# Gate matmuls of two batches as seven block products, and one phase of pairs at the end

## The chip, the core and the metric

The kernel runs on one core of a Trainium2 chip. TensorE (PE; its weight loads are PEld) multiplies into eight PSUM banks; VectorE (DVE), ScalarE (ACT) and GpSimd (POOL) work on SBUF, the first two on PSUM as well; SyncE (SP) issues most transfers. Each engine takes its instructions in the order of its own queue, and a transfer that has to wait holds up those behind it on the queue that issues it. The metric is the time of one execution on the device in microseconds.

## What is computed

The layer works on 32 batches of 512 nodes with 256 channels. With h = relu(layernorm(x)) of one batch:

```python
hc = relu(bn1(conv1(h)))                  # 1x1 convolution over the channels
x_conv = relu(bn2(conv2(hc)) + h)         # 17 taps along the nodes
s = h @ w_se.T + b_se                     # 3 features
A = exp(-dist(s)) * adj
x_nmp = A @ relu(h @ w_msg.T + b_msg)
gi = concat(x_conv, x_nmp) @ w_ih.T + b_ih
gh = h @ w_hh.T + b_hh
r = sigmoid(gi_r + gh_r); z = sigmoid(gi_z + gh_z)
n = tanh(gi_n + r * gh_n)
out = x + (1 - z) * n + z * h
```

The gates are three outputs of 256 channels (r, z, n) from three inputs of 256 channels (h, x_nmp, x_conv). In blocks of 128 channels that is 6 output blocks times 6 input blocks for every batch. Everything is float32.

## The kernel before

The 32 batches are two groups of 16. Conv2 goes through a Fourier transform: each batch is cut into 8 windows, the windows of a group's 16 batches fill 128 rows, and there are 40 `product` units per group that multiply spectra with the transformed taps. The stages, in program order:

- `first_part(0)`: statistics, normalisation, transposition of x to h (`hT`, stored as HD), conv1, forward transform into `xf`; beside it the taps are transformed and stored (WD). The weights of the gates, `wih` and `whh`, are loaded here in six transfers, one per batch.
- nodes of group 0: `message` (`pm`), `features`, `factors` (`psl`, `psr`), `affinity` (`pd`, the exponential, the transposed adjacency `at`, and their product `A`), `aggregate` (`pn`), `save_nmp` (ND). The 40 products of the group (`py`) lie between these steps, two or three per batch.
- `first_part(1)`, the same without the taps. Its order on each engine is the written one. Per batch it takes `rstd` by a power on GpSimd (L237), and it loads x on GpSimd's queue.
- rest of group 0, with the products of group 1 between: per batch the inverse transform (`freq_to_windows`, `pc` at L426), `gates_rz` and `gate_n` (`pg`, `pgh`, `pgi` at L436), `finish` (`po`, the output).
- last phase: for each batch of group 1 the nodes of the next batch and the gates of this one, between each other.

Where the order isn't fixed by hand, a scheduler at build time orders instructions by the program's order and by the buffers that are free. A gate block is one chain of matmuls into a fresh bank: for r and z six of them (two for each of hT, nmp and xconv), for n two and four in two banks. ScalarE takes the sigmoid out of the bank; VectorE and ScalarE make n and the blend. All gate weights stay in SBUF from the first stage on.

In the nodes phases the pool that holds the adjacency and `A` has one buffer of each.

## Time and profile before

| | |
|---|---|
| time, median of 3 runs | 2080.53 us (2076.18 to 2081.81) |
| profiled execution | 2081.35 us, span 2079.6 us |
| granted TensorE clock, mean | 0.988 |
| busy: PE, DVE, ACT, POOL | 2032.1, 909.1, 550.2, 285.9 us |
| stages, roughly from the chain in order of time | first 0 to 184; nodes and products 184 to 505; first 505 to 620; rest and products 620 to 1262; nodes and rest 1262 to 2080 |

A row of instructions gives line, engine, operation, output<-inputs, shapes, count; then busy time and the mean of one in ns, and the idle time of the engine ahead of them with what ended it. A matmul in float32 leaves two rows, so counts of TensorE are twice the number of matmuls. In the timeline a row starts with its start and length in us; in brackets stands the idle time ahead of it and who ended it. Rows of stretches give the busy time and count for PE, PEld, DVE, ACT and POOL, then the granted clock, the share of the DMA engines and GB/s.

### The profile page before, as it was taken

To read this page: it belongs to the slowest core of one execution; us is meant where nothing else is said; L and a number is where in the kernel's file an instruction comes from. 1 tells how busy PE (TensorE), PEld (TensorE's weight loads), DVE (VectorE), ACT (ScalarE), POOL (GpSimd) and SP (SyncE) were. 2 spreads that over 40 slices of the span, in tenths; PEclk is the share of its full clock that TensorE was granted. 3 is DMA by queue.
4 is the path that set the end of the run, shared out by engine and by line. 5 is a ranking of instruction groups with operands and counts; after the bars stand their busy time and mean duration, and the time that the engine had idled before them with its cause. 6 is when DMAs were issued, how large, how long until landed. Compare 5 with 4: busy or idle time off the path is not lost.

```text
span 2079.6 us, 20881 instructions
## 1 busy us (share of the span) xinstructions
PE 2032.1 (98%) x7616; PEld 1231.3 (59%) x7616; DVE 909.1 (44%) x1877; ACT 550.2 (26%) x898; POOL 285.9 (14%) x331
## 2 busy tenths in 40 slices
PE   7989999998999999999999999999999999999998
PEld 5666677675985555655556555555555555555554
DVE  7874666666962222321232223344444333333443
ACT  2544333332342111111111111222223222222231
POOL 2321333333211121221212100000000000000000
PEclk9997999999999999999999999999999999999999
DMA  8997887886554334453435451223333322222200
GB/s 214 320 267 197 231 217 229 237 219 209 170 171 129 123 120 128 144 171 95 131 124 155 144 134 51 50 74 76 84 79 89 86 70 70 70 70 70 70 30 20
DMA packets 222581, 277.47 MB, mean 133 GB/s; under 512 B 12959, under 2 KB 187871, under 8 KB 222479
## 3 DMA queue, kind: packets, MB, share of 16 engines
q1 hardware_dynamic: 205071, 227.30, 39.7%
q10 hardware_dynamic: 12224, 31.86, 4.0%
q0 software_dynamic: 5184, 16.98, 3.1%
q8 instruction: 61, 1.00, 0.2%
q14 instruction: 41, 0.34, 0.1%
HBM read 181.71 MB, written 94.37 MB: 133 GB/s over the span
## 4 chain that ended last, share of the span: by engine, by line
PE 90%; DVE 4%; DMA 2%; issue 1%; ACT 1%; POOL 0%; SPq 0%; DVEq 0%; POOLq 0%; ACTq 0%
PE pg L436 32%; PE pgi L436 11%; PE pn L396 10%; PE py L314 9%; PE pm L348 6%; PE pc L426 5%; PE pgh L436 5%; PE pc L267 3%; PE px L281 2%; PE pd L382 2%; PE po L479 1%; PE pw L212 1%; DVE stats L232 1%; PE phT L254 1%; DMA x<-in_x_dram 1%
## 5 line engine op out<-in xcount | busy, mean ns | idle before, releaser
L436 PE MATMUL pg<-nmp,wih 128*128 128x512 f32 x512 | 240.8, 592 | 0.0
L436 PE MATMUL pg<-hT,whh 128*128 128x512 f32 x512 | 240.6, 592 | 0.0
L436 PE MATMUL pg<-xconv,wih 128*128 128x512 f32 x512 | 240.6, 592 | 0.0
L462 DVE SCALAR_TENSOR_TENSOR n<-pgh,vec,rz 128x512 f32<-128x512 f32 x64 | 47.8, 747 | 428.3 <-PE pgh L436 428.3
L451 ACT ACTIVATE rz<-pg,brz 128x512 f32<-128x512 f32 x128 | 87.9, 687 | 541.3 <-PE pg L436 536.1
L396 PE MATMUL pn<-A,msg 128*128 128x512 f32 x512 | 227.7, 598 | 2.7 <-DVE A L388 2.7
L436 PEld LDWEIGHTS pg<-xconv,wih 128*128 128x128 f32 x512 | 97.3, 190 | 122.5 <-issue 122.5
L436 PEld LDWEIGHTS pg<-nmp,wih 128*128 128x128 f32 x512 | 97.2, 190 | 122.0 <-issue 121.5
L319 DVE COPY y<-py 128x256 f32<-128x256 f32 x78 | 31.5, 418 | 314.6 <-PE py L314 314.4
L396 PEld LDWEIGHTS pn<-A,msg 128*128 128x128 f32 x512 | 96.9, 192 | 120.4 <-issue 113.2
L436 PEld LDWEIGHTS pg<-hT,whh 128*128 128x128 f32 x512 | 97.2, 191 | 108.2 <-issue 104.3
L314 PE MATMUL py<-wt,both 128*128 128x256 f32 x624 | 148.1, 380 | 0.0
L306 POOL TENSOR_TENSOR both<-xf 128x256 f32<-128x256 f32 x78 | 60.6, 776 | 618.7 <-PE py L314 573.4
L387 DVE STREAM_TRANSPOSE at<-adj 128x512 f32<-128x512 f32 x128 | 134.3, 1083 | 10.8 <-DMA adj<-in_adj_dram 10.4
L348 PE MATMUL pm<-wmsg,hT 128*128 128x259 f32 x512 | 132.4, 413 | 0.0
L314 PEld LDWEIGHTS py<-wt,both 128*128 128x128 f32 x624 | 116.8, 190 | 24.6 <-issue 11.3
L348 PEld LDWEIGHTS pm<-wmsg,hT 128*128 128x128 f32 x512 | 123.5, 327 | 13.2 <-issue 11.4
L464 ACT ACTIVATE n<-n,vec 128x512 f32<-128x512 f32 x64 | 46.2, 722 | 318.2 <-DVE n L463 318.2
L426 PEld LDWEIGHTS pc<-back,yt 120*128 120x128 f32 x1024 | 119.5, 192 | 17.7 <-issue 17.7
L436 PE MATMUL pgh<-hT,whh 128*128 128x512 f32 x256 | 121.9, 598 | 0.0
L426 PE MATMUL pc<-back,yt 120*128 120x80 f32 (+1 forms) x1024 | 118.3, 273 | 2.6 <-DMA yt<-yd 2.6
L267 PE MATMUL pc<-w,hT 128*128 128x256 f32 x512 | 119.7, 388 | 0.6 <-DVE hT L255 0.6
(89 smaller groups left out, 2529.4 us busy)
## 6 DMA issues: line engine op xcount, KB each, us to landing
wt<-wd SPq DMA_DIRECT2D x160, 256.0 KB, 5.5
adj<-in_adj_dram SPq DMA_DIRECT2D x128, 256.0 KB, 5.1
yd<-y ACTq DMA_DIRECT2D x80, 384.0 KB, 5.8
yt<-yd SPq DMA_DIRECT2D x64, 480.0 KB, 6.6
hT<-hd SPq DMA_DIRECT2D x48, 512.0 KB, 3.8
wd<-wst SPq DMA_DIRECT2D x64, 320.0 KB, 5.5
x<-in_x_dram SPq DMA_DIRECT2D x38, 512.0 KB, 4.4
hd<-hT SPq DMA_DIRECT2D x32, 512.0 KB, 4.7
```

The source lines that it names most:

```text
L267: nc.tensor.matmul(p[:, j, :], HT[b][:, ic, c * P : (c + 1) * P], w1[:, ic, :], start=(ic == 0), stop=(ic == DC - 1))
L281: nc.tensor.matmul(p[:, j * 2 * L : (j + 1) * 2 * L], H1[b][:, c0 + j, ic * P : (ic + 1) * P], fwd, start=True, stop=True)
L306: nc.gpsimd.tensor_tensor(both[:, 0], re, im, op=ALU.add)
L314: nc.tensor.matmul(dst, v[:, ic, :], w[:, ic, :], start=(ic == 0), stop=(ic == DC - 1))
L348: nc.tensor.matmul(p[:, : D + NS], chunk(HT[b][:, ic, :], c), wmsg[:, ic, :], start=(ic == 0), stop=(ic == DC - 1))
L387: nc.vector.transpose(at.rearrange("p (j k) -> p j k", k=32), ADJ[b].rearrange("p j (q c) -> p c j q", c=NC)[:, mc])
L396: nc.tensor.matmul(p, MSG[b][:, mc, dc * P : (dc + 1) * P], A[b][:, mc, :], start=(mc == 0), stop=(mc == NC - 1))
L426: nc.tensor.matmul(p[:, t0:t1], YT[b][w][:, oc * P : (oc + 1) * P], back[:, u0 : u0 + t1 - t0], start=(w == 0), stop=(w == W - 1), skip_gr ...
L436: nc.tensor.matmul(p, w, v, start=(i == 0), stop=(i == len(terms) - 1))
L451: nc.scalar.activation(RZ[b][:, g, :], p, AF.Sigmoid, bias=brz[:, g : g + 1], scale=1.0)
L462: nc.vector.scalar_tensor_tensor(n, ph, b_hn[:, i : i + 1], RZ[b][:, i, :], op0=ALU.add, op1=ALU.mult)
L464: nc.scalar.activation(n, n, AF.Tanh, bias=b_in[:, i : i + 1], scale=1.0)
```

## The change

Two things change together.

**Gates of a pair.** Two batches are taken together. For one gate (256 output channels) and one source (256 input channels) the weights are 2 x 2 blocks a11, a12, a21, a22, and the operand is 2 x 2 blocks as well: input half by batch, each 128 x 512. Instead of 8 block products the kernel makes the seven of Strassen's method in Winograd's form: four sums of weight blocks (S1 to S4) and four differences of operand blocks take the place of single blocks in them. The products of the three sources h, nmp and xconv go into the same bank one after the other, since their sums are combined in the same way. The combination of the seven is partly done by accumulation: a bank that holds Q1 is copied out (`p1`) and goes on to Q1 + Q2; a bank with Q6 is read (`u2` = Q1 + Q6), goes on to Q6 + Q7, is read again (`u3`), and goes on to Q6 + Q7 + Q4. For n, the part of h and the part of the other two sources stay apart, in two banks each.

The differences of operands are made by GpSimd (`sums`, 4 for each source and pair). The weight sums are made once by GpSimd (`combine_weights`), stored to DRAM (WS), and loaded when the pairs begin.

**Order of the phases.** The nodes of group 1 follow `first_part(1)`, with the 40 products of group 1 spread over its first 13 batches; `save_nmp` stores all 32 batches. After that the early pools are closed, and one phase in written order runs the 16 pairs: load, inverse transform, gates, blend, output. A pair's output lies inside the next pair's `gates_rz`.

```diff
-    load_weights = [partial(nc.sync.dma_start, wih[:, i], w_ihT[i * P : (i + 1) * P]) for i in range(2 * DC)]
-    load_weights += [partial(nc.sync.dma_start, whh[:, i], w_hhT[i * P : (i + 1) * P]) for i in range(DC)]
-    load_weights += [
+    load_weights = [
...
+    def combine_weights():
+        sources = [w_hhT, w_ihT[D:], w_ihT[:D]]
+        for k, src in enumerate(sources):
+            w = pools["sums"].tile([P, DC, G], FP, tag="wraw", name=f"wraw_{k}")
+            nc.sync.dma_start(w, src.rearrange("(c p) o -> p c o", p=P))
+            w = w.rearrange("p c (g i o) -> p c g i o", i=2, o=P)
+            a11, a21, a12, a22 = w[:, 0, :, 0], w[:, 0, :, 1], w[:, 1, :, 0], w[:, 1, :, 1]
+            t = pools["sums"].tile([P, 7, 3, P], FP, tag="wsum7", name=f"wsum7_{k}")
+            for dst, a in ((A11, a11), (A12, a12), (A22, a22)):
+                nc.gpsimd.tensor_copy(t[:, dst], a)
+            nc.gpsimd.tensor_tensor(t[:, S1], a21, a22, op=ALU.add)
+            nc.gpsimd.tensor_tensor(t[:, S2], t[:, S1], a11, op=ALU.subtract)
+            nc.gpsimd.tensor_tensor(t[:, S3], a11, a21, op=ALU.subtract)
+            nc.gpsimd.tensor_tensor(t[:, S4], a12, t[:, S2], op=ALU.subtract)
+            nc.sync.dma_start(WS[k], t)
...
+    def load_pair(p):
+        HP[p] = pools["ops"].tile([P, 8, N], FP, tag="hp", name=f"hp_{p}")
+        NP[p] = pools["ops"].tile([P, 7, N], FP, tag="np", name=f"np_{p}")
...
+            nc.sync.dma_start(HP[p][:, j:4:2], HD[b])
+            nc.sync.dma_start(NP[p][:, j:4:2], ND[b])
...
+                nc.sync.dma_start(t, YD[g][w : w + W // 2].rearrange("w r d -> r w d"))
...
+    def sums(t, keep):
+        t3 = 7 if keep else B12
+        sub = ALU.subtract
+        for dst, a, b in ((4, B12, B11), (5, B22, 4), (6, B21, 5), (t3, B22, B12)):
+            nc.gpsimd.tensor_tensor(t[:, dst, :], t[:, a, :], t[:, b, :], op=sub)
...
+    def into(bk, q, o, ks, terms, first):
+        for i, k in enumerate(ks):
+            nc.tensor.matmul(bk, sw[:, k, q, o, :], terms[k][q], start=(first and i == 0), stop=(i == len(ks) - 1),
+                             skip_group_check=True)
...
+        for o in range(2):
+            b1[o] = bank(f"pg1_{p}_{o}")
+            into(b1[o], Q1, o, ks, terms, True)
+            p1[o] = temp("p1", f"{p}_{o}")
+            nc.scalar.copy(p1[o], b1[o])
+        for o in range(2):
+            b2[o] = bank(f"pg2_{p}_{o}")
+            into(b2[o], Q6, o, ks, terms, True)
+            u2[o] = temp("u2", f"{p}_{o}")
+            nc.vector.tensor_add(u2[o], p1[o], b2[o])
+        for o in range(2):
+            into(b1[o], Q2, o, ks, terms, False)
+            sigmoid(b1[o], o, 0, 0)
+        between(0)
+        for o in range(2):
+            into(b2[o], Q7, o, ks, terms, False)
+            u3[o] = temp("u3", f"{p}_{o}")
+            nc.vector.tensor_add(u3[o], p1[o], b2[o])
+        between(1)
...
+        pair(Q5, x3, True)
+        scaled(x3[0], u3[0], u3[1], 1, 1)
+        closing(x3[1], 1, 1)
+        pair(Q4, x2, False)
+        scaled(x2[0], p1[0], p1[1], 1, 0)
+        closing(x2[1], 1, 0)
+        pair(Q3, x3, False)
+        scaled(x3[0], u2[0], u2[1], 0, 1)
+        closing(x3[1], 0, 1)
+        for i, j in ((0, 0), (1, 1), (1, 0), (0, 1)):
+            blend(i, j)
...
+            with phase("nodes"):
+                nodes(0, xf, GB)
+            with phase("first", "sums"):
+                combine_weights()
                 xf = freq_tile(1)
                 with tc.manual_schedule():
                     first_part(1, xf, lambda i: ([], []))
+            with phase("nodes"):
+                nodes(1, xf, GB - 3)
+    outer.close()
...
+    with phase("late"), phase("sw"), phase("ops", bufs=2), phase("work"), tc.manual_schedule():
+        pairs = B // 2
+        load_pair(0)
+        sw = load_combined()
+        sums(HP[0], True)
+        sums(NP[0], False)
+        inverse(0)
+        sums(CP[0], False)
+        for p in range(pairs):
...
+            gates_rz(p, terms, between)
+            if more:
+                inverse(p + 1)
+                sums(CP[p + 1], False)
+            gate_n(p, terms)
```

`between` holds the two outputs of the pair before, the loads of x for this pair and the sums of h and nmp for the next.

How the instructions move at three places. First, GpSimd at the start of `first_part(1)`; `rstd` and the load of x belong to first_part, `wsum` from `wt` to a product. Before:

```order
L309 TENSOR_TENSOR wsum_2_5305<-wt_2_5297 128x512
L237 TENSOR_TENSOR rstd_4132<-rstd_4132,minus_half 128x4
L99 DMA x_4139<-in_x_dram 128x4x256
L237 TENSOR_TENSOR rstd_4166<-rstd_4166,minus_half 128x4
L99 DMA x_4187<-in_x_dram 128x4x256
```

and now, with the operations of `combine_weights` (from `wraw`):

```order
L311 TENSOR_TENSOR wsum_1_5300<-wt_1_5292 128x512
L425 COPY wsum_0_4101<-wraw_4099 128x384 x3
L426 TENSOR_TENSOR wsum_0_4101<-wraw_4099 128x384
L428 TENSOR_TENSOR wsum_0_4101<-wraw_4099 128x384
L427 TENSOR_TENSOR wsum_0_4101<-wsum_0_4101,wraw_4099 128x384
L429 TENSOR_TENSOR wsum_0_4101<-wraw_4099,wsum_0_4101 128x384
L239 TENSOR_TENSOR rstd_4182<-rstd_4182,minus_half 128x4
L104 DMA x_4189<-in_x_dram 128x4x256
L311 TENSOR_TENSOR wsum_2_5348<-wt_2_5340 128x512
L239 TENSOR_TENSOR rstd_4216<-rstd_4216,minus_half 128x4
L104 DMA x_4237<-in_x_dram 128x4x256
L425 COPY wsum_1_4112<-wraw_4110 128x384 x3
```

The seven operations of a source stand ahead of an rstd and of the load of x behind it; the next source follows two batches later.

Second, TensorE around the nodes of a late batch. Before, in the last phase (`pgh`, `pgi`: gates; `pd`: distances; `pn`: aggregation):

```order
L368 MATMUL psr_8866<-ident,fr 128x128 x4
L436 MATMUL pgh_0_8874<-hT_21_8588,whh 128x512 x2
L436 MATMUL pgi_0_8877<-nmp_8735,wih 128x512 x2
L436 MATMUL pgi_0_8877<-xconv_8748,wih 128x512 x2
L382 MATMUL pd_0_8890<-sr_8871,sl_8864 128x512
L382 MATMUL pd_1_8891<-sr_8871,sl_8864 128x512
L382 MATMUL pd_2_8892<-sr_8871,sl_8864 128x512
L382 MATMUL pd_3_8893<-sr_8871,sl_8864 128x512
L436 MATMUL pgh_1_8918<-hT_21_8588,whh 128x512 x2
L436 MATMUL pgi_1_8921<-nmp_8735,wih 128x512 x2
L436 MATMUL pgi_1_8921<-xconv_8748,wih 128x512 x2
L396 MATMUL pn_0_8934<-A_8889,msg_8797 128x512 x4
```

and now, in the last batches of the second nodes phase:

```order
L384 MATMUL pd_3_7220<-sr_7160,sl_7153 128x512
L350 MATMUL pm_0_7254<-wmsg,hT_30_7245 128x259 x2
L350 MATMUL pm_1_7259<-wmsg,hT_30_7245 128x259 x2
L350 MATMUL pm_2_7265<-wmsg,hT_30_7245 128x259 x2
L350 MATMUL pm_3_7270<-wmsg,hT_30_7245 128x259 x2
L370 MATMUL psl_7281<-ident,fl 128x128 x4
L370 MATMUL psr_7288<-ident,fr 128x128 x4
L398 MATMUL pn_0_7296<-A_7216,msg_7079 128x512 x4
L398 MATMUL pn_1_7302<-A_7216,msg_7079 128x512 x4
L384 MATMUL pd_0_7310<-sr_7293,sl_7286 128x512
```

The gates that stood between the steps of the nodes are gone from there; between a batch's `pd` and its `pn` lie only the next batch's message and the transposes of its factors.

Third, SP where the pairs begin (`nd`: the store of an aggregate; `hp`, `np`, `yt`, `sw`: what the first pair needs); there is no such place before:

```order
L404 DMA nd_201<-nmp_7388 128x1024
L444 DMA hp_7464<-hd_139 128x2x512
L404 DMA nd_202<-nmp_7431 128x1024
L445 DMA np_7465<-nd_171 128x2x512
L444 DMA hp_7464<-hd_140 128x2x512
L445 DMA np_7465<-nd_172 128x2x512
L452 DMA yt_0_7470<-yd_137 120x4x256
L452 DMA yt_1_7472<-yd_137 120x4x256
L452 DMA yt_0_7474<-yd_137 120x4x256
L452 DMA yt_1_7476<-yd_137 120x4x256
L435 DMA sw<-ws_203 128x2688
L435 DMA sw<-ws_204 128x2688
```

The store of the last batch (`nd_202`) stands ahead of all but one of the loads of the first pair, and the weight sums stand last.

323 lines of the change are left out of this document (169 added, 154 removed).

## The prediction

> **What bounds the kernel now.** I read first the page's busy shares and the chain that ended last:
>
> ```profile
> span 2079.6 us, 20881 instructions
> PE 2032.1 (98%) x7616; PEld 1231.3 (59%) x7616; DVE 909.1 (44%) x1877; ACT 550.2 (26%) x898; POOL 285.9 (14%) x331
> PE pg L436 32%; PE pgi L436 11%; PE pn L396 10%; PE py L314 9%; PE pm L348 6%; PE pc L426 5%; PE pgh L436 5%; PE pc L267 3%; PE px L281 2%; PE pd L382 2%; PE po L479 1%; PE pw L212 1%; DVE stats L232 1%; PE phT L254 1%; DMA x<-in_x_dram 1%
> ```
>
> TensorE is busy for all but 47.5 us, and the gates (pg, pgi, pgh) hold 48% of the chain. Next the chain in order of time and the busy time by stretches (PE, PEld, DVE, ACT, POOL, clock, DMA share, GB/s):
>
> ```profile
> 1320.13 20.60 PE pg L436 x48
> 1353.17 6.87 PE pn L396 x16
> 1360.04 3.53 PE pc L426 x32
> 1364.45 3.85 PE pm L348 x16
> 1368.30 20.60 PE pg L436 x48
> ...
> 1320.00:2030.00 710.00, 710.00 (x2336) 379.95 (x2335) 281.03 (x538) 195.15 (x266) 0.00 (x0) 1.00 0.28 70
> 50.00:70.00 20.00, 19.53 (x115) 13.78 (x115) 16.05 (x42) 9.85 (x22) 6.81 (x10) 1.00 1.02 308
> 505.00:522.00 17.00, 10.70 (x49) 7.81 (x48) 13.92 (x41) 1.81 (x3) 4.85 (x5) 0.83 0.70 222
> ...
> HBM read 181.71 MB, written 94.37 MB: 133 GB/s over the span
> ```
>
> In the second half a batch takes 48.2 us (1320.13 to 1368.30) without one idle moment of TensorE, at full clock. Each matmul has two rows, so a gate matmul costs 20.60/24 = 0.858 us. A matmul saved there is time saved, as long as the work that stays is still packed. TensorE idles mostly where stages begin, and the change makes new beginnings: these decide how much of the saving remains.
>
> **The matmuls saved.** Before: 36 gate matmuls per batch (6 output blocks times 6 input blocks), 72 per pair. Now: 7 products, 3 gates, 3 sources = 63. Shape and row length are the same, so 9 x 16 x 0.858 = **-123.6 us**.
>
> **Is the pair phase packed?** Per pair TensorE needs 63 x 0.858 + 2 x 3.53 (inverse) + 16 transposes (1.7) = 62.9 us. The others, by these groups:
>
> ```profile
> L309 POOL TENSOR_TENSOR wsum<-wt 128x512 f32<-128x512 f32 x78 | 100.6, 1290 | 104.4 <-DMA wt<-wd 93.2 <-PE pn L396 11.1 <-DVE msg L351 0.2
> L306 POOL TENSOR_TENSOR both<-xf 128x256 f32<-128x256 f32 x78 | 60.6, 776 | 618.7 <-PE py L314 573.4 <-ACT xf L284 45.2
> L462 DVE SCALAR_TENSOR_TENSOR n<-pgh,vec,rz 128x512 f32<-128x512 f32 x64 | 47.8, 747 | 428.3 <-PE pgh L436 428.3
> L469 DVE TENSOR_TENSOR o<-o,n 128x512 f32<-128x512 f32 x64 | 44.1, 690 | 1.7
> L464 ACT ACTIVATE n<-n,vec 128x512 f32<-128x512 f32 x64 | 46.2, 722 | 318.2 <-DVE n L463 318.2
> ```
>
> GpSimd: 12 sums x 1.29 = 15.5 us. VectorE: 48 operations at 0.69 to 0.75, about 34 us. ScalarE: 20 x 0.72 = 14 us. DMA: 6.2 MB, 98 GB/s against the 308 above. None is near 62.9. The new waits are hand-overs: a product goes into a bank whose partial sum VectorE or ScalarE has just read. Tightest is gate n: the bank pair of Q5 is taken by Q3, with Q4's three matmuls (2.57 us) between, and its readers are four VectorE operations (2.8 us), of which the first can start 1.7 us before Q5 ends; they end about 1.1 us after it. The twelve blends of a pair follow its last product and keep VectorE until about 10 us into the next pair; the next need, Q7 into the bank that u2 frees, comes at 15 us. So I cost the hand-overs at nothing; uncovered, one costs up to the 0.7 us of its reader.
>
> **The beginnings.** These rows price them: the start of the second half, its first `pn`, the start of the first half's gates, and a wait in the first stage.
>
> ```profile
> 1297.11 0.66 PE L368 MATMUL psl<-ident,fl 128*128 128x128 f32 x4 [1.76 <-DVE fl L360]
> 1299.61 2.09 PE L382 MATMUL pd<-sr,sl 9*128 9x512 f32 x8 [1.15 <-ACT sr L373]
> 1303.18 9.52 PE L396 MATMUL pn<-A,msg 128*128 128x512 f32 x16 [1.49 <-DVE A L388]
> 622.80 1.98 PE L426 MATMUL pc<-back,yt 120*128 120x72 f32 x16 [2.63 <-DMA yt<-yd]
> 155.15 1.17 PE L281 MATMUL px<-fwd,h 128*128 128x160 f32 x3 [4.54 <-DVE hT L255]
> 140.28 11.12 DMA x<-in_x_dram
> ```
>
> *What goes:* the start of the rest phase (2.6) and of the second half's nodes (1.76 + 1.15 + 1.49, and a `pn` of 9.52 instead of 6.87, 2.65, at a granted clock below 1): **-9.7**.
>
> The Trainium skill, page "TensorE: Matmul & The Clock Gate", section "Part 1: The HAM clock gate", halves the clock only after an idle window of about 3.4 us. Here three waits of under 2 us brought the slow `pn`, so the row is taken; by the page three longer waits would cost 1.7 us each, an estimate, and the sum would be about 2 us lower.
>
> *First stage:* the six loads of gate weights (6 x 384 KB = 2.36 MB, 7.7 us at 308 GB/s) leave a stretch where the DMA engines are full and a load of x is waited for. Between 0 and -10 (the wait of 4.54 and the slow clock behind it); **-6**.
>
> *Second first_part:* `combine_weights` puts three rounds of 7 GpSimd operations ahead of rstd, which every normalisation needs, and of the x loads queued on GpSimd; each round waits for its load, and the next load for the store of the last sums.
>
> ```profile
> 509.90 1.26 POOL L309 TENSOR_TENSOR wsum<-wt 128x512 f32<-128x512 f32 x1 [8.89 <-DMA wt<-wd]
> 511.27 1.02 POOL L237 TENSOR_TENSOR rstd<-rstd,minus_half 128x4 f32<-128x4 f32 x1
> 522.45 1.04 POOL L237 TENSOR_TENSOR rstd<-rstd,minus_half 128x4 f32<-128x4 f32 x1 [3.23 <-DVE rstd L236]
> 535.39 1.04 POOL L237 TENSOR_TENSOR rstd<-rstd,minus_half 128x4 f32<-128x4 f32 x1 [4.72 <-DVE rstd L236]
> 510.10 1.09 DVE L236 TENSOR_SCALAR rstd<-mv 128x4 f32<-128x4 f32 x1
> L236 DVE TENSOR_SCALAR rstd<-mv 128x4 f32<-128x4 f32 x32 | 6.3, 198 | 1.0
> ```
>
> An operation on 384 elements lies between 0.78 and 1.29, about 1.03. Copies have no row: between 0.3 (a third) and 1.03; I take the addition's. Round one (7.2 us) fits before 511.3 if its load, issued near 497, is there. Store and load are 2.16 MB, 7.0 us at 308 GB/s, with issue and landing 8.5: with its six first operations (6.2) round two ends near 525.7, and the rstd of 522.45 is 3.2 late; round three makes the one of 535.39 another 4.6 late. Bounds: 0 (first_part keeps a batch ahead) and 20 (round one late by its 7, and VectorE held as at 510.10, where 0.2 became 1.09 until GpSimd ended). **+8**.
>
> The Trainium skill, page "SBUF — State Buffer", section "Who interferes with whom", says a VectorE operation in a two-port mode and a GpSimd operation exclude each other for a whole instruction; the 1.09 row agrees. By it all 21 sums could each hold VectorE, 21 x 0.9 = 19 us, the second rival below.
>
> *Start of the second nodes:* the same sequence that cost 7.05 at 1297. **+7** (4 to 12).
>
> *Nodes without products:* group 1 spreads its 40 products over 13 batches; the last three have none.
>
> ```profile
> L387 DVE STREAM_TRANSPOSE at<-adj 128x512 f32<-128x512 f32 x128 | 134.3, 1083 | 10.8 <-DMA adj<-in_adj_dram 10.4 <-issue 0.2
> L388 DVE TENSOR_TENSOR A<-e,at 128x512 f32<-128x512 f32 x128 | 84.6, 699 | 31.3 <-ACT e L385 31.0
> L385 ACT ACTIVATE e<-pd 128x512 f32<-128x512 f32 x128 | 73.0, 596 | 79.1 <-PE pd L382 51.8 <-DVE A L388 16.9 <-PE pm L348 6.9
> L351 DVE TENSOR_TENSOR msg<-pm,bmsg 128x256 f32<-128x256 f32 x128 | 52.4, 416 | 3.7 <-DMA wd<-wst 3.7
> ...
> adj<-in_adj_dram SPq DMA_DIRECT2D x128, 256.0 KB, 5.1
> ```
>
> Before, gate matmuls lie between `pd`, `pm` and `pn`. Without them, from the end of `pd`: exp 0.75, four A multiplications with two transposes between, 5.35; then the next message's additions and features on VectorE, 7.8. TensorE has only `pm` (3.9): it waits 3.9 us, a batch later 4.9 (its first transposes stand behind the `nmp` copies), and in the last batch, with nothing of a next one, 3.2; clock 4. **+16** (8 to 24). The single adjacency buffer is reloaded (5.1 us to land) while VectorE does the message, and is late for nobody.
>
> *Start of the pairs:* the save of the last batch waits on SP for its copy, and behind it stand np, hp, np (1.57 MB), four yt (1.97) and three weight sums (4.13): 7.67 MB, 24.9 us at 308 GB/s, 27 with copy and landing. TensorE does the inverse (7.1) and two products (1.7) meanwhile; with 2.65 of clock **+21**. From 7 (as at 622.80, weights hidden) to 31 (at 222 GB/s).
>
> *Tail:*
>
> ```profile
> 2067.85 1.88 PE L436 MATMUL pgi<-xconv,wih 128*128 128x512 f32 x4
> 2072.76 0.69 DVE L469 TENSOR_TENSOR o<-o,n 128x512 f32<-128x512 f32 x1
> 2073.51 1.54 PE L479 MATMUL po<-ident,o 128*128 128x128 f32 x6 [3.56 <-DVE o L469]
> 2074.45 1.33 DVE L481 TENSOR_TENSOR x<-x,po 128x512 f32<-128x512 f32 x2 [1.00 <-PE po L479]
> out_dram<-x SPq DMA_DIRECT2D x32, 512.0 KB, 3.3
> ```
>
> Last product to end: 9.9 us now, of which three blends. Then: rest of the closings and 12 blends 10.1, transposes and additions 2.6, output 3.3 = 16: **+6** (4 to 9).
>
> **Sum.** -123.6 - 9.7 - 6 + 8 + 7 + 16 + 21 + 6 = -81.3: span 1998.3. The profiled execution took 2081.35, 1.75 over its span, so 2000.1; the median of the runs is 0.8 below that execution. I say **2000 us**.
>
> **Rivals.**
> (1) *Hand-overs stall, slower than before.* 14 per pair (7 in rz, 7 in n), 224 in all. From 81.3/224 = 0.36 us each the gain is gone. A hand-over without cover cost 1.15 (`pd` after ACT sr); at half of it, 0.6, the time is 2000 + 134 = 2134. Against it: the covers above. 5%.
> (2) *GpSimd holds the second first_part:* 19 + 20 instead of 8, 2031. For it the row at 510.10; against it, GpSimd is mostly idle there. 8%.
> (3) *The pair phase is paced by loads.* SP's loads of the next pair wait for the blends (10 us in) that free the hidden states' buffer, and bring 4.07 MB: 13.2 us at 308 GB/s, landed at 25. The inverse needs them at 37.8 (42 matmuls and 16 transposes), the sums, 8 x 1.29 on GpSimd, a pair's end later. That fails where the loads take over 26.5 us, below 154 GB/s; at 133 they are 4.1 us late, 15 times, 2062. For it: 133 is the mean over the span. Against it: that mean is demand, and the full stretches moved 222 and 308. 7%.
> (4) *The beginnings are cheaper:* combine 0, first stage -10, nodes 8, pairs 7, start 4: 2000 - 37 = 1963. 15%.
> (5) *The products don't keep 0.858* (accumulating on a read bank has no row): at 0.90, 1008 x 0.042 = 42, 2042. 5%.
>
> My forecast has 60%, its own range 1980 to 2025. For 8 in 10 I reach into (4), (2) and (5): 1968 to 2044. Only (1) is slower. With 0.3% (6 us, what a measurement here tells from no change): faster 0.94, same 0.01, slower 0.05.
>
> **What would show it.** 2016 gate rows (1008 matmuls) at 0.858 us a pair of rows; pairs every 62.9 us, TensorE full between the first and last; waits of 3 to 5 us before three `psl`/`pn` near the end of the second nodes, some 18 us idle before the first complete product, and the rstd of batches 19 and 21 late by 3 to 8 us. Wrong would be a pair period above 64 us, or idle time of TensorE inside the pairs named after VectorE, ACT or DMA.

## The result, and the profile after

| | median | range |
|---|---|---|
| before | 2081.17 us (4 runs) | 2076.18 to 2082.91 |
| after | 2006.0 us (4 runs) | 2004.61 to 2009.42 |

The ratio is 0.9645, with a 95% interval of 0.9624 to 0.9666: 3.5% faster, 75 us. The profiled execution took 2009.42 us with a span of 2007.6, 72.0 under the span of before. The forecast was 2000, from 1968 to 2044.

The head of the page of the changed kernel, and the two groups that carry the gates (busy us and share, then rows; in a group busy time, mean ns, idle time ahead):

```profile
span 2007.6 us, 21238 instructions
PE 1929.0 (96%) x7328; PEld 1188.8 (59%) x7328; DVE 1158.1 (58%) x2197; ACT 546.3 (27%) x930; POOL 541.7 (27%) x544
...
L492 PE MATMUL pg<-hp,sw 128*128 128x512 f32 x448 | 229.8, 595 | 0.0
L492 PE MATMUL pn<-hp,sw 128*128 128x512 f32 x224 | 115.1, 595 | 0.0
```

448 and 224 rows for each of three sources are 2016, or 1008 matmuls, as many as were to be. These groups show no idle time of TensorE ahead of them (0.0). VectorE went from 909.1 to 1158.1 and GpSimd from 285.9 to 541.7 without coming near the span.

The chain in order of time shows the pair phase as a period (start, length, what):

```profile
1053.11 15.45 PE pg L492 x36
...
1116.08 15.45 PE pg L492 x36
```

62.97 us a pair, and so on to the last. The same stretch and those ahead of it, by windows (PE, PEld, DVE, ACT, POOL busy; granted clock; DMA share; GB/s):

```profile
505.00:522.00 17.00, 8.47 (x39) 6.20 (x37) 10.31 (x27) 1.82 (x3) 8.29 (x10) 0.82 0.87 302
...
905.00:964.00 59.00, 49.09 (x154) 28.23 (x152) 29.20 (x60) 13.85 (x22) 1.27 (x1) 0.88 0.37 101
964.00:990.00 26.00, 14.52 (x65) 14.23 (x66) 2.97 (x5) 2.17 (x3) 11.28 (x9) 0.55 0.98 315
1053.00:1934.70 881.70, 881.70 (x2886) 458.45 (x2885) 456.39 (x673) 190.96 (x280) 210.93 (x168) 1.00 0.32 98
1972.50:2007.60 35.10, 22.27 (x59) 10.79 (x57) 23.68 (x35) 4.67 (x7) 0.00 (x0) 0.81 0.09 31
```

Fourteen pairs at full clock without an idle moment; what is lost lies at the beginnings. By the prediction's terms, against the span:

| term | forecast | measured | from |
|---|---|---|---|
| 144 gate matmuls | -123.6 | -122.5 | 62.97 a pair for 62.9 of work |
| beginnings that go | -9.7 | -9.7 | they are gone |
| first stage | -6 | 0 | last `pn` of the first nodes starts at 496.96 for 496.71 (rows below) |
| second first_part | +8 | +10.1 | from that `pn` to the end of the last `px`: 133.6 for 123.5 |
| start of second nodes | +7 | +8 | 630.5 to 685: 4.6 idle, 3.4 of slow clock |
| nodes without products | +16 | +16 | 909.0 to 963.7 with 38.9 of work at full clock |
| start of pairs | +21 | +21 | 963.7 to 1027.9 with 43.1 of work |
| tail | +6 | +7 | last product to end 17.0 for 9.9 |
| sum | -81 | -70 | the spans differ by 72.0 |

Work at full clock is counted with the lengths that the same rows have in the packed stretches (`pn` 6.87, `pm` 4.05, the inverse 7.10, a gate row 0.429). The sum comes out to within 2 us, so nothing large is unaccounted for. Two of the terms by their rows: the last `pn` of the first nodes in the chain before and in the chain now, and the third of the waits at the start of the second nodes (the first two, 1.05 and 1.20, come where they came before).

```profile
496.71 6.87 PE pn L396 x16
```

```profile
496.96 6.87 PE pn L398 x16
```

```profile
671.90 0.63 PE L370 MATMUL psl<-ident,fl 128*128 128x128 f32 x4 [2.38 <-DVE fr L364]
...
672.80 8.73 PE L398 MATMUL pn<-A,msg 128*128 128x512 f32 x16
```

The runs below ask four things: whether the products alone are worth 124, whether the hand-overs were close to costing something, why the first stage gave nothing, and what really sets the length of the beginnings.

One thing on how the runs are read. Where the first stage was not touched, the last `pn` of the first nodes started anywhere from 491.8 to 500.8 in ten profiled executions of the changed kernel and its variants. Effects of a few us are therefore read from the length of their own stage. Times are given as ratios to the kernel before, run on the same chip (0.9645 for the change; 0.001 is 2.1 us); the interval of a ratio is some 4 us either way, so a difference of less than that between two ratios shows nothing by itself.

### The profile page after: what moved, and what is told of

Its sections match the earlier page's. It is cut to its first block, busy times and chain, and to the rows that moved or that the text cites. A ratio compares the mean times of both kernels' runs of the same rounds, so it can differ in the third digit from the quotient of the medians.

```text
span 2007.6 us, 21238 instructions
## 1 busy us (share of the span) xinstructions
PE 1929.0 (96%) x7328; PEld 1188.8 (59%) x7328; DVE 1158.1 (58%) x2197; ACT 546.3 (27%) x930; POOL 541.7 (27%) x544
## 4 chain that ended last, share of the span: by engine, by line
PE 87%; DVE 6%; DMA 4%; issue 2%; ACT 1%; POOL 1%; SPq 0%; DVEq 0%; POOLq 0%; ACTq 0%
PE pg L492 29%; PE pn L492 14%; PE pn L398 11%; PE py L316 9%; PE pc L481 6%; PE pm L350 6%; PE pc L269 3%; PE px L283 2%; DMA wd<-wst 2%; PE pd L384 2%; PE po L615 1%; PE pw L214 1%; DVE x L245 1%; DVE stats L234 1%; PE phT L256 1%
## 5 line engine op out<-in xcount | busy, mean ns | idle before, releaser
L492 PE MATMUL pg<-hp,sw 128*128 128x512 f32 x448 | 229.8, 595 | 0.0
L492 PE MATMUL pg<-np,sw 128*128 128x512 f32 x448 | 229.7, 594 | 0.0
L492 PE MATMUL pg<-cp,sw 128*128 128x512 f32 x448 | 229.2, 593 | 0.0
L470 POOL TENSOR_TENSOR hp<-hp 128x512 f32<-128x512 f32 x64 | 80.5, 1268 | 476.3 <-DMA hp<-hd 268.9
L470 POOL TENSOR_TENSOR cp<-cp 128x512 f32<-128x512 f32 x64 | 80.5, 1268 | 296.2 <-ACT cp L486 294.9
L507 ACT ACTIVATE rz<-rz,brz 128x512 f32<-128x512 f32 x96 | 69.2, 721 | 298.7 <-DVE rz L511 298.7
L492 PEld LDWEIGHTS pg<-cp,sw 128*128 128x128 f32 x448 | 85.4, 191 | 107.7 <-issue 107.5
L492 PEld LDWEIGHTS pg<-np,sw 128*128 128x128 f32 x448 | 85.4, 191 | 107.7 <-issue 107.0
L350 PEld LDWEIGHTS pm<-wmsg,hT 128*128 128x128 f32 x512 | 124.3, 327 | 25.3 <-issue 22.0
L492 PEld LDWEIGHTS pg<-hp,sw 128*128 128x128 f32 x448 | 83.0, 191 | 92.6 <-issue 89.0
L311 POOL TENSOR_TENSOR wsum<-wt 128x512 f32<-128x512 f32 x78 | 101.6, 1302 | 124.4 <-DMA wt<-wd 120.7
L481 PE MATMUL pc<-back,yt 120*128 120x80 f32 (+1 forms) x1024 | 123.2, 284 | 11.8 <-DMA yt<-yd 11.6
```

Source lines behind the costliest of these rows:

```text
L311: nc.gpsimd.tensor_tensor(wsum, wr, wi, op=ALU.add)
L350: nc.tensor.matmul(p[:, : D + NS], chunk(HT[b][:, ic, :], c), wmsg[:, ic, :], start=(ic == 0), stop=(ic == DC - 1))
L470: nc.gpsimd.tensor_tensor(t[:, dst, :], t[:, a, :], t[:, b, :], op=sub)
L481: nc.tensor.matmul(bk[:, t0:t1], YT[p][j * W + w][:, oc * P : (oc + 1) * P], back[:, u0 : u0 + t1 - t0], start=(w == 0), stop=(w == W - 1) ...
L492: nc.tensor.matmul(bk, sw[:, k, q, o, :], terms[k][q], start=(first and i == 0), stop=(i == len(ks) - 1), skip_group_check=True)
L507: nc.scalar.activation(rz[:, g, j, :], src, AF.Sigmoid, bias=brz[:, g : g + 1], scale=1.0)
```

## Experiments

### Are the products worth what the matmuls cost?

The pairs compute every gate block from its six blocks, in the same place of the program:

```diff
-        for o in range(2):
-            b1[o] = bank(f"pg1_{p}_{o}")
-            into(b1[o], Q1, o, ks, terms, True)
...
+        for at, (i, j) in enumerate(((0, 0), (1, 1), (1, 0), (0, 1))):
+            for o in range(2):
+                g = 2 * o + i
+                bk = bank(f"pg_{p}_{g}_{j}")
+                blocks(bk, o, i, j, range(K3), terms)
+                nc.scalar.activation(rz[:, g, j, :], bk, AF.Sigmoid, bias=brz[:, g : g + 1], scale=1.0)
```

> The order of the program is kept, but the pairs compute their gates by the eight block products of the definition: 72 matmuls of 512 columns a pair and bank instead of 63, no sums of operands on GpSimd (the sums of weights are still made and stored, but the pairs load the plain weights). Theory: the products alone are worth 9 x 16 x 0.858 = 123.6, all of it on the path, and the reordering of the program costs about 50: pairs every 70.7 us instead of 62.97, the whole at 2127 (the start and the tail are a few us shorter). Rival: the products, with their hand-overs and sums, cost something that the row of 0.858 doesn't show; then taking them out costs less than 123: a pair under 70, the whole under 2115.

Contrary to this text GpSimd's sums of operands were still made, and one of them overwrites an operand block that the plain products read: the time is that of 72 plain matmuls beside the same work of GpSimd, while the values are not those of the definition. Measured: 2126.11 us, ratio 1.0213 [1.0191, 1.0234]. The chain of waits of this kernel:

```profile
1054.38 20.60 PE pg L495 x48
...
1125.08 20.60 PE pg L495 x48
```

A pair takes 70.70, that is 7.73 more than 62.97; 16 of them are 123.7, and the term of 123.6 stands to the decimal. The total is 118 above the changed kernel, less than 124, since the start of the pairs is 2.3 us shorter with plain weights and the tail 1.2. Without the products, then, the new order of the program costs 2.1%, 44 us over the kernel before: the products pay for the reordering and leave 75.

### How close were the hand-overs?

Four more multiplications on VectorE, ahead of the readers of Q5's banks in gate n:

```diff
+        for i in range(4):
+            hold = temp("hold", f"{p}_{i}")
+            nc.vector.tensor_mul(hold, rz[:, 0, 0, :], rz[:, 0, 1, :])
         scaled(x3[0], u3[0], u3[1], 1, 1)
```

> In gate n of each pair, VectorE does four more multiplications of 128x512 (0.69 each, 2.76) ahead of the readers of Q5's banks; nothing reads them. In the profile of the changed kernel the last of these readers ended at 1238.20, and the matmul that takes its bank started at about 1239.3: a cover of 1.1. Theory: what goes past the cover shows, 1.7 us a pair, 16 pairs: +27, 2033, the wait named on PE's pn after VectorE. Rival one: every us that a reader is late shows: +44, 2050. Rival two: other slack takes it up: 2006.

Measured: 2016.37 us, ratio 0.968 [0.9657, 0.9703], 7 us above the change by the ratios instead of 27 (8 by its stages). The pair takes 63.33 (1048.08 to 1111.41 in its chain), 0.36 more, 5.8 for 16, and the tail is 2.2 longer. Its timeline shows why so little (VectorE's rows, then TensorE's):

```profile
1230.63 2.49 DVE L597 TENSOR_TENSOR hold<-rz 128x512 f32<-128x512 f32 x4
1233.04 0.74 DVE L560 SCALAR_TENSOR_TENSOR nt<-pn,vec,u_n 128x512 f32<-128x512 f32 x1
...
1235.34 0.69 DVE L566 TENSOR_TENSOR nt<-nt,pn 128x512 f32<-128x512 f32 x1
...
1234.97 1.02 PE L492 MATMUL pn<-hp,sw 128*128 128x512 f32 x2
1236.08 1.12 PE L492 MATMUL pn<-np,sw 128*128 128x512 f32 x2
```

The four took 2.49, of which 0.34 fell into time in which VectorE had waited for Q5 anyway; the readers came 2.15 later. The matmul that needs the bank of the last reader (L566, done at 1236.03) is not the first of Q3, which goes into the other bank, but the second, from `np`. In the changed kernel without the delay it starts at 1240.15, and the reader is done at 1238.20: a cover of 1.95, not 1.1 as the expectation had it. So 0.2 to 0.4 a pair show. The theory that only what passes the cover costs stands; my reading of the cover was wrong. This hand-over, the tightest in the timeline of a pair, had 1.95 us to spare, nearly three VectorE operations, so the first rival was nowhere near.

### What did the first stage wait for?

The expected gain of 6 from the gate weights' loads did not come. The chain has the same wait as before:

```profile
139.83 11.16 DMA x<-in_x_dram
```

and VectorE's timeline shows who was held up by it (the stretch from 145):

```profile
145.33 0.41 DVE L234 BATCH_NORM_STATS2 stats<-x 128x6 f32<-128x256 f32 x1
151.01 0.43 DVE L234 BATCH_NORM_STATS2 stats<-x 128x6 f32<-128x256 f32 x1 [5.26 <-DMA x<-in_x_dram]
```

Between the two operations stands a load that this stage doesn't need. The order on VectorE there is:

```
L234 BN_STATS stats_15_1553<-x_15_1451 128x6
L234 BN_STATS stats_16_4141<-x_16_4135 128x6
L235 BN_AGGR mv_15_1554<-stats_15_1553 128x2
```

Batch 16 opens the second group. Its statistics were moved ahead, into the gaps of batch 15's, and its x comes by SP's queue, once the buffer of batch 13 is free. One more buffer for x:

```diff
-        X[b] = pools["work"].tile([P, NC, D], FP, tag="x", name=f"x_{b}", bufs=3)
+        X[b] = pools["work"].tile([P, NC, D], FP, tag="x", name=f"x_{b}", bufs=4)
```

> One more buffer for x (4 instead of 3), nothing else. Theory: the wait of the first stage (11.16 us of a load of x from 139.83, TensorE idle 4.57 before px and slow behind it) is for batch 16, the first of the second group, whose statistics stand on VectorE between those of batch 15; its load stands on SP's queue until the buffer of batch 13 is free. With a fourth buffer it is issued a batch (10 us) earlier, the wait goes, and with it 4.6 idle and about 6 of slow clock: the first pn of the nodes starts near 220 instead of 230.3, and the whole takes about 1996 instead of 2006. Rival (the prediction's): the DMA engines are full there and any load of x is late; then the wait stays and the time is 2006 within 2.

Measured: 2000.71 us, ratio 0.9603 [0.9587, 0.9619]. SP issues the load at 129.73, ten us earlier, and the wait of `px` is gone from the list of TensorE's waits in the first stage. The last `pn` of the first nodes starts at 489.05, 7.9 earlier than in the changed kernel and 4.7 below the median of the ten with three buffers (493.8). So the cause is shown, and its size is 5 to 8. The DMA engines are fuller than they were (0.92 from 130 to 160, 0.77 in the changed kernel). The load itself was slow as well: from its issue to its landing it took 11.2 us, where the median load of x takes 5.5. But the loads of x in this stretch take 7.4 to 10.9 in this run too, and nobody waits for them, because they are issued ten us earlier; and the 2.36 MB of gate weights have no part in it, since the load took 11.12 with them and 11.16 without. The expected 1996 was missed, in part because the second first_part was 136.4 long in this execution (133.6 in the changed kernel); the reason is found below, in the section on the start of the pairs.

### Why did the second first_part get longer?

TensorE's wait for normalisation in this stage, before and now (total, times, longest):

```profile
PE phT L254 <- DVE x L243: 5.9, 2, 4.3
```

```profile
PE phT L256 <- DVE x L245: 13.6, 4, 6.3
```

That is 7.7 more of idle time; the other 2.4 of the 10.1 are the lower clock behind these waits. GpSimd's timeline in the changed kernel, behind it VectorE's rows of normalisation (L245), and last the first of them before (L243):

```profile
509.18 1.41 POOL L425 COPY wsum<-wraw 128x384 f32<-128x384 f32 x3 [7.53 <-DVE stats L234]
...
514.47 1.02 POOL L239 TENSOR_TENSOR rstd<-rstd,minus_half 128x4 f32<-128x4 f32 x1
...
522.33 1.03 POOL L239 TENSOR_TENSOR rstd<-rstd,minus_half 128x4 f32<-128x4 f32 x1 [4.74 <-DVE rstd L238]
...
524.12 1.55 POOL L425 COPY wsum<-wraw 128x384 f32<-128x384 f32 x3
...
547.66 1.04 POOL L239 TENSOR_TENSOR rstd<-rstd,minus_half 128x4 f32<-128x4 f32 x1
...
515.52 3.19 DVE L245 TENSOR_SCALAR x<-x,mv,rstd 128x256 f32<-128x256 f32 x4 [4.91 <-POOL rstd L239]
523.39 5.28 DVE L245 TENSOR_SCALAR x<-x,mv,rstd 128x256 f32<-128x256 f32 x4
532.17 2.90 DVE L245 TENSOR_SCALAR x<-x,mv,rstd 128x256 f32<-128x256 f32 x4
...
548.74 2.42 DVE L245 TENSOR_SCALAR x<-x,mv,rstd 128x256 f32<-128x256 f32 x4 [2.71 <-POOL rstd L239]
```

```profile
512.33 1.48 DVE L243 TENSOR_SCALAR x<-x,mv,rstd 128x256 f32<-128x256 f32 x4 [1.13 <-POOL rstd L237]
```

Round one delayed the rstd of batch 17: normalise waited 4.91 for it, 1.13 before. Round two delayed none (GpSimd waited for VectorE there, 4.74 and 2.57 ahead of the next two). Round three delayed the rstd of batch 21, for which normalise waited 2.71, but TensorE had work meanwhile and was idle for only 0.2. And the normalisation beside the first two rounds took 3.19, 5.28 and 2.90 for four instead of 1.46 (beside round three 2.42, off the path). On the path that is 3.8 for round one and 7.0 for the held normalisation, measured on VectorE. The statistics (0.39 to 0.41) and the copies out of PSUM (L257, 1.28 for two) kept their length beside the same sums.

The Trainium skill, page "SBUF — State Buffer", section "Who interferes with whom", has VectorE and GpSimd share a pair of ports as an exclusive lock, taken by operations in a two-port mode and by those with two inputs in SBUF, but by none with at most one SBUF input outside such modes. The trace agrees: normalise, an operation of one SBUF input that may run in such a mode, went from 0.36 to as much as 1.3 each, the others not at all.

Two runs take GpSimd out of this stage. In one the rounds move to the second nodes:

```diff
-                combine_weights()
...
+                if g == 1 and b - b0 in (3, 5, 7):
+                    combine_weights([(b - b0 - 3) // 2])
```

> The three rounds of gate-weight sums move from the second first_part into batches 19, 21 and 23 of the second nodes. Theory: the 10.1 us that the second first_part got longer are the rstd of batch 17 that stood behind round one (about 4) and the normalise operations of VectorE that were held while GpSimd summed (3.19, 5.28 and 2.90 for four instead of 1.46: 7 in all). Both go: the last px ends 123.5 us after the pn before it instead of 133.6, normalise is back at 421 ns on average, and in the nodes the sums lie beside TensorE: about 1996. Rival one: it is the traffic of the weight loads and stores (6.5 MB), which goes with them: gain under 3, 2003 or more. Rival two: in the nodes GpSimd's 7 us a round make the sums of the products late; then TensorE waits for wsum there, up to 7 a round, and the gain is eaten: 2006 to 2015.

Measured: 2002.16 us, ratio 0.9618 [0.9604, 0.9633]. The second first_part is back at 124.3 (501.00 to 625.26) and normalise at 422 ns, as the theory had it. But the rounds did not go where the edit put them: their buffers were free from the start, and the scheduler moved all three into the first stage (sums at 25.6, 54.3 and 80.2), where the third made an rstd 5.4 late and TensorE wait 4.9. Half of the gain went there. In the other run, VectorE and ScalarE do the sums, one addition a batch:

```diff
-            for dst, a in ((A11, a11), (A12, a12), (A22, a22)):
-                nc.gpsimd.tensor_copy(t[:, dst], a)
-            nc.gpsimd.tensor_tensor(t[:, S1], a21, a22, op=ALU.add)
...
+                for dst, a in ((A11, a11), (A12, a12), (A22, a22)):
+                    steps.append(partial(nc.scalar.copy, t[:, dst], a))
...
+            steps.append(partial(nc.vector.tensor_tensor, t[:, dst], a, c, op=op))
```

> The sums of the gate weights stay in the second first_part, with the same loads and stores, but are spread over batches 17 to 29, one addition a batch on VectorE (12 in all) and the 9 copies on ScalarE; GpSimd does none. Theory: the 10.1 us were GpSimd's (rstd behind round one, normalise held while it summed); VectorE has about 1 us a batch free, so the additions lie beside TensorE: the last px ends 124 to 125 us after the pn before it instead of 133.6, normalise at 421 ns on average, 1997 in all. Rival: it was the 6.5 MB of loads and stores, which stay: 2004 or more.

Measured: 1999.5 us, ratio 0.9604 [0.9583, 0.9625].

```profile
DVE wsum L662 <- DMA wraw<-in_w_ihT_dram: 7.3, 2, 3.8
L245 DVE TENSOR_SCALAR x<-x,mv,rstd 128x256 f32<-128x256 f32 x60 | 21.7, 423 | 1.4 <-POOL rstd L239 1.1
```

Normalise is at 423 ns with all 6.5 MB still moving, so it was GpSimd and not the traffic. The stage took 130.2, not 124 to 125: I had issued each load one batch ahead of its use (6.5 us), it landed in 9.3 to 9.5, and VectorE waited for two of the three, 3.8 and 3.5. With the loads two batches ahead (in the run of all edits below) the stage is 124.2. That the time came close to the expected 1997 is chance: the stage gained 3.4, and in this execution the first stage was 3.0 shorter.

### The nodes without products

```diff
-                nodes(1, xf, GB - 3)
+                nodes(1, xf, GB)
```

> The 40 products of the second group are spread over all 16 batches of its nodes instead of the first 13. Theory: the three waits without products (3.21, 4.08, 2.35) and the lowered clock behind them (pn 7.7, 8.6 and 8.8 instead of 6.9) go but for about 3 us in the last batch: -12, 1994. Rival: the products that come late keep their buffers and their loads of wt in the way of the pairs' first loads, which start later by up to 8: 2002 or more.

Measured: 1993.77 us, ratio 0.9569 [0.9543, 0.9595], 16 below the change by the ratios; the profiled executions differ by 12.3. TensorE's waits from 900 on, in the changed kernel and then in this one:

```profile
PE pc L481 <- DMA yt<-yd: 11.6, 1, 11.6
PE psl L370 <- DVE fr L364: 7.3, 2, 4.1
PE pn L398 <- DVE A L390: 2.3, 1, 2.3
```

```profile
PE pc L481 <- DMA yt<-yd: 11.7, 1, 11.7
PE psl L370 <- DVE fr L364: 0.9, 1, 0.9
```

The second nodes take 322.5 from the last `px` to TensorE's last row instead of 333.2, with `pn` back at 6.87 in the last batches, and the first pair starts no later for it (63.0 to the end of its r and z products, 64.2 in the changed kernel). Of the 15.8 us that this place cost, 13.6 are gone; the stage gained only 10.7, since its start was 2.7 longer in this execution (the third wait there is 3.89 for 2.38).

### The start of the pairs

The term of 21 came out to the microsecond, but not as it was put together. I had 18 us of idle time and 2.65 of slow clock; the trace has 11.6 of idle time and 9.3 of slow clock. TensorE's timeline in the changed kernel, then windows (the clock is the third number from the end):

```profile
975.33 2.00 PE L481 MATMUL pc<-back,yt 120*128 120x72 f32 x8 [11.60 <-DMA yt<-yd]
977.48 12.22 PE L481 MATMUL pc<-back,yt 120*128 120x80 f32 x56
```

```profile
968.00:970.00 2.00, 0.00 (x0) 0.00 (x0) 0.00 (x0) 0.00 (x0) 0.00 (x0) 0.50 0.91 271
988.00:990.00 2.00, 2.00 (x10) 1.93 (x10) 0.26 (x1) 0.00 (x0) 1.18 (x1) 0.50 1.01 427
994.00:996.00 2.00, 2.00 (x6) 0.82 (x5) 0.00 (x0) 0.59 (x1) 2.00 (x2) 1.00 1.00 374
```

The inverse takes 14.2 instead of 7.1, and the first products lose another 2.2. Is it the loads or the clock that ends last? Fewer loads:

```diff
+                load_combined(consts, (0,))
                 nodes(1, xf, GB - 3)
...
-        sw = load_combined()
+        load_combined(pools["sw"], (1, 2))
```

> The combined weights of one of the three sources (1.38 MB) are loaded during the second nodes into a place of their own; the other two as before. Theory: the start of the pairs is paced by its 7.67 MB at about 315 GB/s; 1.38 MB less brings the first product 4.4 us forward: from 989.7 to 985, 2001.6 in all. Rival: it is paced by the latency of the last save and by the inverse at the lowered clock (12.2 us for 7.1); then the first product stays within 1 us, 2006.

Measured: 2006.26 us, ratio 0.9634 [0.9617, 0.9651]. From the last `pn` to the end of the first r and z products 63.1 instead of 64.2: the 4.4 did not come (in seven executions that did not touch this place the stretch is 62.8 to 64.2). And the clock:

```diff
+        hot = bank("hot")
+        for i in range(13):
+            nc.tensor.matmul(hot, ident, ident[:, None, :].to_broadcast([P, N // P, P]), start=True, stop=True)
         inverse(0)
```

> While TensorE waits 11.6 us for the first pair's loads it does 13 matmuls of 512 columns on the identity (11.2 us), which nobody reads. Theory: the granted clock, 0.5 from 968 to 994 in the changed kernel, stays at 1; the inverse takes 7.1 instead of 14.2 and the first products lose no 2.2, but the last of the weights lands near 989 (7.67 MB from 964.5 at 315 GB/s), so that some of the 9 is waited for again: -4, 2002; between 1999 and 2004. Rival: the first pair is paced by its loads alone, and a faster inverse only waits longer: 2006.

Measured: 2006.9 us, ratio 0.9632 [0.9605, 0.966]; the same stretch 64.2. The clock stayed at 1.00 to 990 and the inverse was through at 985, but then:

```profile
PE pg L492 <- DMA sw<-ws: 4.2, 2, 2.2
```

the first products waited for the weights, and behind those waits the clock fell to 0.5 after all. Two chains end at the same time here, the loads in the order in which SP issues them and the inverse at half clock; each edit shortened one. Both together, with the products' loads ahead of the others:

```diff
+        if p:
+            halves(HP[p], HD)
+            halves(NP[p], ND)
...
+        if not p:
+            halves(HP[p], HD)
+            halves(NP[p], ND)
```

> Start of the pairs, three edits together: the weights of one source come during the second nodes (as in the run that had this alone), the four loads of the first pair's products go ahead of its hidden states and messages, and 7 matmuls of 512 columns (6 us, read by nobody) keep TensorE busy until they land. Theory: two chains end at the same time there, the loads (991.5 for the last weights where the clock was kept) and the wait of 11.6 with an inverse at half clock (989.7), so that each edit alone gave nothing; together the loads end 4.4 earlier and the inverse near 980: the first product starts 4 to 5 earlier, and the first products keep the full clock (2.2): -6, 2000. Rival: the loads are slower in this order (the rows of the products are short), or something else holds the first product: 2005 or more.

Measured: 2003.12 us, ratio 0.9623 [0.9605, 0.9642]. The stretch is 59.6, 4.6 shorter (6 were expected), with the whole inverse at full clock and 5.4 of waiting for the weights left. By the ratios the time is 4.6 lower as well, but the two intervals overlap. In the profiled execution it is hidden, since the second first_part took 136.5 for 133.6. VectorE's row and then TensorE's show why:

```profile
553.90 2.41 DVE L245 TENSOR_SCALAR x<-x,mv,rstd 128x256 f32<-128x256 f32 x4 [2.72 <-POOL rstd L239]
```

```profile
555.09 0.30 PE L256 MATMUL phT<-ident,x 128*128 128x128 f32 x1 [1.48 <-issue]
```

It is the rstd of batch 21 again, behind GpSimd's third round: here TensorE waits 1.48 and 0.34 for it, and the granted clock falls to 0.5 for 3.4 us. In the run with the fourth buffer the same wait is 1.53, with the same fall, and that stage takes 136.4. In the changed kernel TensorE lost 0.2 there and kept its clock. The early load of weights stands on SP's queue in this stage too, but the run with the fourth buffer has no such load.

The last run asks about the clock by itself: six matmuls of 512 columns on the first landed products, ahead of the inverse.

```diff
+        still = ident[:ROWS, None, :].to_broadcast([ROWS, N // P, P])
+        for i in range(6):
+            nc.tensor.matmul(hot, YT[0][0][:, :P], still, start=True, stop=True)
         inverse(0)
```

> A look at the clock alone: behind the wait of 11.6 us, 6 matmuls of 512 columns that use the first loaded products (read by nobody) stand ahead of the inverse, whose matmuls have 72 and 80 columns. In the changed kernel the granted clock stayed at 0.5 through 14.2 us of that inverse and came back 4.5 us after the first products of 512 columns had begun. Theory: matmuls of few columns don't bring the clock back, those of 512 do within 4 to 5 us: the 6 take 7 to 8 us (three at 1.72, the rest at 0.86), and the inverse then runs at full clock, 7.1. Rival: the clock comes back after some 18 us, whatever TensorE does: the 6 take 10.3 and the inverse still over 10.

One run, 2001.69 us. Its chain:

```profile
969.50 7.67 PE hot L737 x12
977.17 7.10 PE pc L481 x64
984.27 36.10 PE pg L492 x84
```

6 matmuls in 7.67, then the inverse in 7.10 and the products at full clock (36.04 is 84 rows at 0.429). With work that nobody reads the start took 61.8, where it took 62.8 to 64.2 in the seven executions without an edit at this place. That is 1 to 2.4 shorter, in one run.

### The tail, and all together

```diff
+            eng = nc.gpsimd if last and i == j else nc.vector
-            nc.vector.tensor_sub(d, HP[p][:, 2 * i + j, :], n)
+            eng.tensor_tensor(d, HP[p][:, 2 * i + j, :], n, op=ALU.subtract)
...
         closing(x1[1], 0, 0)
+        if last:
+            blend(0, 0)
```

> In the last pair alone the blends of two of the four blocks are done by GpSimd right behind their tanh; the other two stay on VectorE at the end, the block that the first output needs first. Theory: the tail is VectorE's row of 12 blends behind the last product (8.3 us); half of them gone and GpSimd's three at 1.3 each earlier done: the end comes 4 us earlier, 17.0 from the last product becomes 13, 2002. Rival: GpSimd's operations hold VectorE's as they did in the second first_part, and the closings come late by as much: 2006.

Measured: 2002.43 us, ratio 0.9618 [0.9601, 0.9635]. From the last `pg` to the end 33.9 for 35.1: 1.2 of the 4. That the time is near the expected 2002 is chance: in this execution the first stage was 3.7 shorter. The rival had the rest of the 4:

```profile
1979.58 1.80 DVE L561 TENSOR_TENSOR nt<-nt,rz 128x512 f32<-128x512 f32 x1
...
1982.21 0.69 DVE L566 TENSOR_TENSOR nt<-nt,pn 128x512 f32<-128x512 f32 x1
...
1984.32 1.64 DVE L562 TENSOR_TENSOR nt<-nt,p_n 128x512 f32<-128x512 f32 x1
...
1979.57 1.27 POOL L575 TENSOR_TENSOR nt<-nt,rz 128x512 f32<-128x512 f32 x1
1983.73 1.68 POOL L573 TENSOR_TENSOR rz<-hp,nt 128x512 f32<-128x512 f32 x1 [2.90 <-ACT nt L567]
```

Three of VectorE's operations with both inputs in SBUF took 1.52 to 1.80 for 0.69, 2.9 in all; those with an input in PSUM (L560, L566) kept their 0.69 to 0.75. All edits at once:

> All edits that the runs point to, together: the fourth buffer for x, products over all 16 batches, the weight sums on VectorE and ScalarE (their loads issued two batches ahead instead of one, since VectorE waited 7.3 us for them), the three edits at the start of the pairs, and two blocks of the last blends on GpSimd. Theory: the terms lie at different places and add up: 8 (first stage) + 14 (nodes) + 10 (second first_part) + 6 (start of pairs) + 4 (tail) = 42 under 2006: 1964. Rival: what is gained ahead of the start of the pairs is lost there, since it is paced by loads that wait for the last batch: 1975 or more.

Measured: 1974.62 us (5 runs, 1972.78 to 1976.75), ratio 0.9481 [0.9467, 0.9495]: 34 us faster than the change, 5.2% faster than before. By stages against the changed kernel's trace: first stage 7.1 (489.87), second first_part 9.4 (124.2), second nodes 13.4 (319.8), start of pairs 4.6 (59.6), the rest in the tail; the spans differ by 35.9. The terms do add up; the start and the tail gave 4.6 and about 1 where 6 and 4 were expected, and so the time was 10 above the expected 1964. It is the rival's 1975, but not by the rival's mechanism: nothing gained ahead of the start of the pairs was lost there.

## Why the prediction was right, and where it was not

**Matmuls saved** and **hand-overs at nothing.** Both held. 123.6 was measured as 123.7 by the run with plain products; the tightest hand-over had 1.95 us of cover. Rivals 1, 3 and 5 fall with the window of 881.70 busy out of 881.70: no stall, no wait for loads, and the gate rows at 592 to 595 ns, as in the run with plain products.

**First stage, -6: wrong, 0.** The step that failed is the inference from a stretch where the DMA engines are full and a load of x is waited for to the six weight loads as its cause. It never asked which x was waited for and when it was issued. The load was batch 16's, behind the buffer of batch 13, and its wait is independent of 2.36 MB that passed earlier: VectorE waited for it as long with them as without (5.2 and 5.3). The total of this stage is less sure than the wait, since there is one trace of before, at 496.7, and the ten with the change have a median of 493.8; a gain of up to 3 by something else is not excluded. Rows on their own don't name buffer numbers; the order of the instructions does, and it was there to be read.

**Second first_part, +8: right in size (10.1), wrong in its mechanism.** The step put the loss on the rstd of batches 19 and 21, late by 3.2 and 4.6 behind rounds two and three. The one of batch 19 was not late; the one of batch 21 was, by 2.8, but cost TensorE 0.2 (and about 3 in two of the other executions, with the clock). What cost most was what the step had as its upper bound: round one ahead of an rstd (3.8) and VectorE held while GpSimd sums (7.0). The row at 510.10 was quoted but taken for an exception. The second rival, which had this mechanism at 39, was right in kind and four times too dear: it let each of 21 sums hold VectorE, while nearly all of the holding fell on normalise, and that of four batches met the sums.

**Nodes without products, +16: right (16).** The place and the cause were right, and the run that spreads the products took the waits away. The parts were each off by 2, and that they cancel is luck: the three waits were 3.21, 4.08 and 2.35 for 3.9, 4.9 and 3.2, and the slow clock behind them cost 6 for 4 (4.1 in `pn`, 2.0 in the transposes ahead of it).

**Start of the pairs, +21: right in sum by luck, wrong in its parts.** TensorE was thought idle for 18 and slow for 2.65. It was idle for 11.6 and slow for 9.3, because the clock did not come back during the inverse. The weights, which the step took for the limit, landed in the shadow of that: they were the second of two limits that end together, as the runs that moved one of them each showed.

**Start of the nodes (+8 for +7), tail (+7 for +6).** The tail came as worked out. At the start of the nodes the first two waits are those of the row, but the third stands a batch later, ahead of the second `psl` instead of the first `pn`: VectorE got to its features late there, behind a multiplication for A that took 1.75 us for 0.68 beside a GpSimd sum of 1.72.

The fourth rival, cheaper beginnings, asked for a first stage 10 shorter and sums at nothing: neither came. In the profiled execution the span misses the forecast by 9.3. The terms account for 11: 6 from the first stage, 2 from the second first_part, 1 each from the pairs, the second nodes' start and the tail. The median lies 3.4 under that execution and so misses by 6.

## What to carry to other kernels

Before a wait for a load is put down to traffic, find out which buffer's load it is, when it was issued and what stood ahead of it: here the last stage's reader was a batch of the next group, pulled forward by the scheduler. Work given to an idle GpSimd is free only while VectorE reads from PSUM or makes statistics; the operations that work from SBUF alone, normalise with one input and sums and products with two, waited until GpSimd's were over. In the pair phase GpSimd's twelve sums meet none of these, and VectorE's products from two SBUF inputs (L561, L573) take 691 to 693 ns in all 112 rows. And when two edits at a start each give nothing, two chains may end there together: count both before either is called harmless.

## What the runs showed of the hardware

In the changed kernel the granted clock fell to 0.5 some 2.8 us after TensorE stopped at 963.7 (1.00 from 964 to 966, 0.64 from 966 to 968, 0.50 from 968). Then it stayed there for the 18.5 us from 975.3 to 993.9 in which TensorE was busy: through 14.2 us of matmuls of 72 and 80 columns and another 4.4 of 512 columns. In the nine other profiled executions that ran the first inverse at the lowered clock, 9.5 to 14 us of it did not bring the clock back either; it came back 1.7 to 5.0 us after the first product of 512 columns. Six matmuls of 512 columns ahead of the inverse brought it back in about 4.6 us (three of them at 1.72), and the inverse that followed kept it. In the run of all edits a wait of 2.26 us was enough: the clock fell 3.6 us after that wait had begun, with TensorE already back on the narrow matmuls. In the kernel before, a wait of 2.63 us ahead of the same narrow matmuls (at 622.80) did not lower it. So narrow matmuls keep a full clock (the pair phase holds 1.00 through every inverse) but were not seen to bring one back. The Trainium skill, page "TensorE: Matmul & The Clock Gate", section "Part 1: The HAM clock gate", gives a window of about 3.4 us both ways, counted in time and not in matmuls. The clock records agree with the window: the stretches between two changes of the clock are multiples of 3.41 us (966.55 to 993.86 is eight of them). The 14.2 us of narrow matmuls without effect, and the fall after a wait of 2.26, don't agree with it.
